# A Fourier neural operator and a dilation on one core: fc1 and fc2 of the head dealt out separately, and the fold, the rows and the first bursts in a new order

## The chip, the cores and the metric

The kernel runs on one core of one Trainium2 chip. The metric is device time in microseconds of one launch. PE is the matrix engine, DVE the vector engine, ACT the scalar engine, POOL and SP the engines that here mostly issue DMAs.

## The reference

The input x is eight images of 8 channels and 256 x 256 pixels, float32 throughout. Two layers, each with a residual:

```
x = x + conv(groupnorm(x))        # layer A: a grouped Fourier neural operator
x = x + dilate(groupnorm(x))      # layer B: the maximum over 3 x 3, padded with -2
```

`conv` has G = 4 groups. Two channels of a group and two coordinate planes go through a 1 x 1 convolution (fc0) to 10 channels. Four layers follow, each with a spectral convolution (rfft2, the lowest 12 x 12 modes mixed over channels, low and high rows apart, irfft2) plus a 1 x 1 convolution; the first three end in a swish. The head is fc1 (10 to 128 channels of a group), swish, fc2 (128 to 2).

## The kernel before

Images run one after the other. For an image, each of the four layers l = 0 to 3 is made of these stages:

- `spectrum_h`: the spectrum from the row transforms of the layer before (four DVE transposes, then the matmuls `p_b`). For layer 0 it is `spectrum_x`, on the raw image.
- `mix`: twelve DVE steps that multiply with the spectral weights (`load_sw`) and reduce, in pairs; then six short DVE operations fill `fs`, the fold's matmuls (`p_f`) fold the rows and DVE copies the result into `fz`.
- `rows_of`: three row groups (`p_g`), whose results DVE copies into `zt`.
- `layer`: eleven bursts (`p_z`), one for each chunk of the image: 48 instructions on PE that add the 1 x 1 convolution and the inverse transform of the columns, then two ACT passes that put swish of it into `h` (for l = 3 without swish; then the chunk also goes to HBM as `stored`). In layers 0 to 2 the new `h` is at once transformed for the next layer: `turn` (DVE transposes, two halves of a chunk), `transform` (64 matmuls `p_d` for two chunks, emptied by DVE and ACT) and `gather` (`p_u`, copied by DVE into `zt`).

The head reads `stored` back. It has 128 steps an image: `first(n)` is fc1 of 512 pixels (four matmuls in the program, eight instructions in the trace, then ACT passes of 512 and 1536 columns into one `act` buffer), and `second(n)` is fc2 of the two steps n and n + 1 (16 instructions into one bank), whose sum DVE adds to the image in `add`. The adds wait in `sums_due` until `sum_up` writes them out. After the last `add` of an image its dilation (`dilate`, or `dilate_last` for the last image) follows as tails.

The order on PE, DVE, ACT and SP is written by hand: it is the order in which the Python program issues instructions. `layers` is a generator that yields at chosen places, and the loop over the images puts work of the previous image's head or dilation there. Each head is a generator too: one `step()` of it is a `first(n)` and, when n is odd and over 2, `second(n - 3)`. A yield of `(1,)` deals one step and writes its add at once, `(1, 1)` two, `"late"` one step with the add left for the next, and `"tail"` a piece of the dilation. The head of an image thus runs beside the next image; the last image's head runs alone, with the dilation of the image before. The spectrum and mixing of layer 0 of the next image (`start`) are drawn piece by piece with `next(side, None)` during layer 3, and what is left of them is yielded by `rest`.

PSUM is shared by all through two tags, and a buffer is given again when all that read it are done:

```python
def ps_a(name):
    return ps.tile([128, 512], F32, tag="one", bufs=2, name=name)
def ps_tri(name):
    return ps.tile([128, 3, 512], F32, tag="tri", bufs=2, name=name)
```

`ps_four` takes one of each. A burst, a `first`, a `transform`, a fold and the first row group take both; the other row groups and the statistics of the dilation (`p_st_y`, `p_sv_y`) take a tri; `second`, `gather` and the rest take a one. The results of `first` go to four buffers:

```python
act = sb.tile([128, G, 512], F32, tag="act", bufs=4, name=f"act_{b}_{n}")
```

Image 0 has no head beside it (`alone[0]`), and there `copy` puts every second copy of `rows_of` on ACT.

Of the kernel before, what the change touches and what calls it, by code (L numbers as in the profile page):

```python
# [33 lines left out]
NBLK = 3  # L34
NCH = 11
NQ = 4
# [3 lines left out]
DR = 2  # L40
STEPS = 128


@with_exitstack
def fno_dilate_kernel(ctx: ExitStack, tc: tile.TileContext, a: dict, out: bass.AP):
# [304 lines left out]
    def spectrum_h(b, l, out_):  # L350
# [3 lines left out]
        for g in range(G):  # L354

            nc.vector.transpose(  # L356
                rows[:, 960 * g : 960 * (g + 1)].rearrange("p (i r) -> p i r", r=32), windows(g))
            yield (1,)
        yield (1,)
        p = ps_a(f"p_b_{b}_{l}")  # L360
# [25 lines left out]
    def mix(b, l, out_):  # L386
# [3 lines left out]
        for n in range(12):  # L390
# [5 lines left out]
            else:  # L396
# [25 lines left out]
        if l == 0:  # L422
            mr = out_["mr"]
            nc.vector.tensor_tensor(dc[:, 0:1], mr[:, 0:1], mr[:, 1:2], ALU.mult)
            out_["wcn"] = sb.tile([128, 32], F32, tag="wcn", bufs=1, name=f"wcn_{b}")
            nc.vector.tensor_scalar(out_["wcn"], wc, mr[:, 1:2], None, ALU.mult)
            for r in range(4):
                mm(one[part(r), n_f : n_f + NO * G], dc, wm[:, NO * r : NO * (r + 1), :], start=True, stop=True)
            nc.vector.tensor_tensor(
                fz[:, :, :, 24], one[:, n_f : n_f + NO * G].rearrange("p (o g) -> p o g", o=NO), cz[:, 0], ALU.add)  # L430
        else:
            nc.vector.tensor_copy(fz[:, :, :, 24], cz[:, l])
        if l < 2:
            nc.vector.tensor_copy(fz[:, :, :, 25], cz[:, 4 if l == 0 else 3])
        cols = fz.rearrange("p o g c -> p (o g) c")
        nc.vector.tensor_copy(
            cols[:, :, 0:6].rearrange("p x c -> p c x"), one[:, :n_f].rearrange("p (c x) -> p c x", c=6))
        for q in range(1, 4):
            nc.vector.tensor_copy(
                cols[:, :, 6 * q : 6 * q + 6].rearrange("p x c -> p c x"),  # L440
                tri[:, q - 1, :n_f].rearrange("p (c x) -> p c x", c=6))

    def rows_of(b, l, side):

        zv = zt[:, :, :, : NBLK * WID].rearrange("p r f (n o) -> p o n r f", n=NBLK)
        yield (1, 1)
        for oi in range(NO):
            name = f"p_g_{b}_{l}_{oi}"
            if oi == 0:
                banks = ps_four(name)[2]  # L450
            else:
                tri = ps_tri(name)
                banks = [tri[:, r, :] for r in range(3)]
# [4 lines left out]
            else:  # L458
                for g in range(G):
                    for j in range(NQ):  # L460
                        for r, p in enumerate(banks):
                            mm(p[part(j), NBLK * CS * g : NBLK * CS * (g + 1)], fz[part(r), oi, g, :],  # L462
                               rowg[part(r), :, j, :], start=True, stop=True)
            for r, p in enumerate(banks):
                src = p[:, : NBLK * CS * NQ]
                if l % 2 == 0:
                    dst = zv[:, NO * r + oi].rearrange("p n r f -> p n f r")
                    src = src.rearrange("p (n f r) -> p n f r", n=NBLK, r=CS)
                else:
                    dst = zv[:, NO * r + oi].rearrange("p n r f -> p f n r")  # L470
                    src = src.rearrange("p (f n r) -> p f n r", f=NQ, n=NBLK)
                copy(r, dst, src)
# [13 lines left out]
    def layer(b, l, out_, stored, side):  # L486
# [89 lines left out]
        for k in range((NCH + 1) // 2):  # L576
# [5 lines left out]
            if alone[0]:  # L582
# [5 lines left out]
                if pair:  # L588
                    turn(c + 1)
                continue  # L590
            if k == 1:
                transform(0)
            if k > 0:
                yield (1,)
            else:
# [15 lines left out]
        transform(k)  # L611
        yield (1,)
        gather(k)
# [7 lines left out]
    def rest(b, then):  # L621
        c = 0 if b == 0 else NCH - 4
        for n in then:
            yield n
# [78 lines left out]
    def head(b, stored, stats):  # L703
        hs, acts, box = {}, {}, {}
        last = b + 1 == n_img
# [22 lines left out]

        def first(n):

            sum_up()
            k, blk = n // 32 * NCH + n % 32 // NBLK, n % 32 % NBLK
            act = sb.tile([128, G, 512], F32, tag="act", bufs=4, name=f"act_{b}_{n}")
# [6 lines left out]

        def second(n):

            t, rb = n // 16, n % 16
            if rb == 8:
# [25 lines left out]

        load_state(0)
        yield
        load_state(1)
        load_y(0)
        yield
        load_state(2)
        yield
        for n in range(STEPS):
            if n % 32 % NBLK == 0:
                load_state(n // 32 * NCH + n % 32 // NBLK + 3)  # L780
            first(n)
            if n % 2 and n > 2:
                second(n - 3)
            yield
        second(STEPS - 2)
        sum_up()

# [58 lines left out]
    with tc.manual_schedule(engines={PE, DVE, ACT, SP}):  # L846
# [3 lines left out]
        for b in range(n_img):  # L850
            stored = [dram.tile([128, NQ * PIX], F32, tag=f"hs{c}", name=f"stored_{b}_{c}") for c in range(NCH)]
            ahead, new = {}, None
            for n in layers(b, stored, d, start(b + 1, ahead)):
                if n == "ready":
                    if new is None:
# [4 lines left out]
                        new = head(b, stored, stats_of[b])  # L860
                    next(new)
                elif n == "stored":
                    heads.append((b, new))
                    alone[0] = False
                elif n == "tail":
                    tail()
                elif heads:
                    for _ in range(1 if n == "late" else len(n)):
                        step()
                        if n != "late":  # L870
                            sum_up()
            d = ahead
        while step():
            sum_up()
            tail()
# [168 lines left out]
```

## Time and profile before

| what | us |
|---|---|
| median of three runs (lowest to highest) | 3849.73 (3849.6 to 3853.38) |
| the profiled execution, its own time | 3850.84 |
| span of the profiled execution, first to last instruction | 3849.0 |
| first row group of images 1, 2, 3, 4, 5, 6, 7 starts at | 357, 812, 1275, 1734, 2194, 2658, 3115 |
| last burst of layer 3 of image 7 starts at | 3546 |
| last fc2 starts at | 3820 |

An image in the middle takes about 460 us. Image 0 alone takes the first 340 us, the last image's head alone some 275, and DVE's last dilation and the output the rest. The mean granted clock of PE in the whole execution was 0.972. Line numbers in the views are those of the kernel before: L736 is fc1 and L751 fc2, L737 and L738 the two ACT passes of fc1, L542 and L545 the two halves of a burst, L550 and L552 its ACT passes, L510 transform, L524 gather, L493 turn, L760 the add. In the changed kernel fc1 is L752, fc2 L769 and the ACT passes L753 and L754.

### The profile page before, as it was taken

The numbers are of one execution on the slowest core, as the hardware profiler recorded it, in microseconds if no ns is written. First come the engines' busy times: TensorE is split into PE (matmuls) and PEld (weight loads), VectorE is DVE, ScalarE is ACT, GpSimd is POOL, SyncE is SP. The second block draws the span as 40 slices with busy tenths as digits, with TensorE's granted clock in tenths as the row PEclk, the third lists the DMA queues.
The fourth block names the chain that finished last, engine by engine and source line by source line (L and its number), as shares of the span: only waits on it lengthen the run. The fifth ranks groups of instructions, "written<-read, shape, count | busy, mean of one in ns | idle before, by whom it ended". The sixth has DMA issues, their size and how long they took to land.

```text
span 3849.0 us, 119276 instructions
## 1 busy us (share of the span) xinstructions
PE 3620.7 (94%) x54200; PEld 1347.2 (35%) x54200; DVE 2423.8 (63%) x3893; ACT 2832.3 (74%) x2919; POOL 117.0 (3%) x202
## 2 busy tenths in 40 slices
PE   5668999999999999999999999999999999999997
PEld 2333333333333333333333333333333333333222
DVE  6775665556775666766666676665676566673633
ACT  2435777777777777787777777777777777778986
POOL 1000000000000000000000000000000000000100
PEclk7878999999999999999999999999999999999998
DMA  3005111432225222361123612144222532225321
GB/s 88 15 28 193 48 47 45 150 107 61 65 85 178 77 61 61 99 200 55 49 64 110 193 56 58 44 145 154 61 63 59 178 99 63 65 64 182 114 54 51
DMA packets 114089, 345.11 MB, mean 90 GB/s; under 512 B 15984, under 2 KB 18480, under 8 KB 98160
## 3 DMA queue, kind: packets, MB, share of 16 engines
q1 hardware_dynamic: 95392, 276.32, 23.4%
q0 software_dynamic: 18192, 61.17, 5.0%
q8 instruction: 426, 6.98, 0.7%
q14 instruction: 79, 0.65, 0.1%
HBM read 213.43 MB, written 123.74 MB: 88 GB/s over the span
## 4 chain that ended last, share of the span: by engine, by line
PE 76%; DVE 14%; issue 5%; ACT 4%; DMA 1%; POOL 0%; DVEq 0%; POOLq 0%; ACTq 0%
PE p_fc L736 20%; PE p_fc L751 19%; PE p_z L545 10%; PE p_d L510 8%; PE p_z L542 8%; PE p_u L524 3%; PE p_z L539 3%; DVE S L397 3%; DVE turned L394 3%; PE p_b L366 2%; DVE y L760 2%; PE p_g L462 2%; ACT act L738 2%; DVE turned L356 1%; ACT act L737 1%
## 5 line engine op out<-in xcount | busy, mean ns | idle before, releaser
L738 ACT ACTIVATE act<-p_fc 128x1536 f32<-128x1536 f32 x1024 | 1492.6, 1458 | 36.1 <-PE p_fc L736 35.0
L736 PE MATMUL p_fc<-hs,c_w 32*128 32x512 f32 x8192 | 1227.4, 633 | 49.9 <-ACT act L738 13.5
L751 PE MATMUL p_fc<-act,c_w 128*32 128x512 f32 x8192 | 996.1, 602 | 2.0 <-issue 2.0
L737 ACT ACTIVATE act<-p_fc 128x512 f32<-128x512 f32 x1024 | 615.4, 601 | 360.1 <-PE p_fc L736 347.0
L493 DVE STREAM_TRANSPOSE turned<-h 128x1024 f32<-128x1024 f32 x528 | 633.9, 1226 | 250.7 <-ACT h L550 249.9
L550 ACT ACTIVATE h<-p_z 128x512 f32<-128x512 f32 (+1 forms) x528 | 511.9, 1022 | 265.4 <-PE p_z L545 265.4
L736 PEld LDWEIGHTS p_fc<-hs,c_w 32*128 32x128 f32 x8192 | 388.1, 185 | 666.4 <-ACT act L737 230.2
L760 DVE TENSOR_TENSOR y<-p_fc,y 128x512 f32<-128x512 f32 x392 | 267.1, 681 | 551.2 <-PE p_fc L751 551.2
L751 PEld LDWEIGHTS p_fc<-act,c_w 128*32 128x32 f32 x8192 | 215.6, 109 | 713.3 <-issue 376.3
L545 PE MATMUL p_z<-c_binv,zt 32*128 32x256 f32 x5632 | 415.5, 410 | 0.4
L542 PE MATMUL p_z<-h,c_wt 32*32 32x512 f32 x8448 | 367.3, 604 | 6.1 <-ACT act L737 4.2
L545 PEld LDWEIGHTS p_z<-c_binv,zt 32*128 32x128 f32 x5632 | 261.6, 189 | 312.8 <-issue 296.6
L510 PE MATMUL p_d<-turned,c_fw 32*32 32x480 f32 (+1 forms) x9216 | 308.6, 540 | 4.3 <-PE p_z L545 2.9
L514 ACT ACTIVATE turned<-p_d 128x1440 f32<-128x1440 f32 x144 | 182.9, 1270 | 95.2 <-PE p_d L510 92.0
L552 ACT ACTIVATE h<-p_z,c_bias 128x512 f32<-128x512 f32 (+1 forms) x176 | 186.5, 1110 | 76.0 <-PE p_z L545 75.8
L207 DVE COPY zt<-p_g 128x264 f32<-128x264 f32 x304 | 154.7, 604 | 76.6 <-PE p_g L462 46.5
L397 DVE TENSOR_REDUCE S<-turned 128x80 f32<-128x800 f32 x192 | 188.8, 983 | 5.7
L394 DVE TENSOR_TENSOR turned<-t,B 128x800 f32<-128x800 f32 x192 | 188.4, 981 | 0.1
L510 PEld LDWEIGHTS p_d<-turned,c_fw 32*32 32x32 f32 x9216 | 128.2, 103 | 170.2 <-issue 65.1
L356 DVE STREAM_TRANSPOSE turned<-zt 128x960 f32<-128x960 f32 x96 | 177.0, 1870 | 2.9 <-DVE zt L527 0.5
L542 PEld LDWEIGHTS p_z<-h,c_wt 32*32 32x32 f32 x8448 | 92.4, 103 | 188.8 <-ACT act L737 66.6
L524 PE MATMUL p_u<-turned,c_stack 128*32 128x480 f32 (+1 forms) x1152 | 136.7, 543 | 7.2 <-DVE turned L513 6.2
(182 smaller groups left out, 1742.8 us busy)
## 6 DMA issues: line engine op xcount, KB each, us to landing
stored<-h SPq DMA_DIRECT2D x88, 1024.0 KB
hs<-stored SPq DMA_DIRECT2D x352, 256.0 KB
t<-in_spw SPq DMA_DIRECT2D x96, 400.0 KB
yin<-y_rows POOLq DMA_DIRECT2D x56, 512.0 KB, 5.2
h<-in_xp SPq DMA_DIRECT2D x352, 48.0 KB
turned<-in_xw SPq DMA_DIRECT2D x16, 1024.0 KB
y<-in_x SPq DMA_DIRECT2D x56, 256.0 KB
y_rows<-y POOLq DMA_DIRECT2D x56, 256.0 KB, 3.9
```

What stands on the lines that cost most here:

```text
L394: nc.vector.tensor_tensor(pr, sw[k], bt[:, k2, k].unsqueeze(2).to_broadcast([128, G, 2 * WID, WID]), ALU.mult)
L397: nc.vector.tensor_reduce(s[k2][:, k].rearrange("p s o g -> p (s o) g"), pr.rearrange("p g m i -> p m g i"), AX.X, ALU.add,)
L493: nc.vector.transpose(dst[:, 2 * i : 2 * i + 2], h[:, c, 2 * i : 2 * i + 2].rearrange("p f (s x) -> p f s x", s=2))
L510: mm(banks[q][part(v % 4), : 240 * n], fw8[part(q), v, :], t[part(q), :, :, v, : NBLK * WID], start=v < 4, stop=v >= 4)
L542: mm(o, wt[part(q), l, g, :], h[part(q), c, f, :], start=True, stop=False)
L545: mm(banks[q][:, HW * s : HW * (s + 1)], zt[part(q), 2 * c + s].rearrange("p f o -> p (f o)"), binv[part(q), :], start=False, stop=s == 1)
L550: nc.scalar.activation(dst, src, AF.Silu)
L736: mm(banks[g], w1[part(g), blk, :], hs[k][part(g), :], start=True, stop=True)
L737: nc.scalar.activation(act[:, 0, :], one, AF.Silu)
L738: nc.scalar.activation(act[:, 1:4, :], tri, AF.Silu)
L751: mm(acc[part(g), :], w2[:, g, 15 - rb - i : 47 - rb - i], act[:, g, :], start=i == 0, stop=i == 1)
L760: nc.vector.tensor_tensor(y, sums, y, ALU.add)
```

## The change

What is dealt out is now a letter: `f` is one `first`, `c` one `second` with its add at once, `C` one `second` with its add left for the next `first`, and `t` a tail. A yield is a string of them. `head` returns functions and counters in place of a generator, and `step(kind)` goes to the first head in the list that still has work of that kind, so that at the switch `first` of the next image may come before the last `second` of the one before. The yields are written anew in `spectrum_h`, `mix`, `rows_of`, `layer` and `rest`. In `mix` and the fold one pair of fc1 and a fc2 now come before the fold's matmuls, the copies of `cz` go ahead of them, and three copies into `fz` become one. In `rows_of` the first row group's copies begin with the tri. In `layer`, bursts, turns and transform 0 of chunks 0 to 3 stand in another order. In layer 3, a chunk's letters are `ft` and `fc`. When all layers of the last image are done, the loop deals `f`, `f`, `c` and a tail until no head is left.

```diff
+REST = ("ff", "f", "f", "fC", "fc"), ("fC", "ffC", "ffC", "f", "fc")
...
# spectrum_h
-            yield (1,)
-        yield (1,)
+            yield "f" if g % 2 else "fc"
+        yield "fc"
# mix
-            if n not in (2, 6, 10) if l > 0 else n % 2 or n > 7:
-                yield "late"
+            if l == 0:
+                if n % 2 or n > 7:
+                    yield
+            elif n not in (2, 6, 10):
+                yield "fC" if n in (1, 4, 7, 9) else "f"
...
-        if l == 0:
-            yield "late"
+        yield "fc"
...
+        if l > 0:
+            nc.vector.tensor_copy(fz[:, :, :, 24], cz[:, l])
+        if l < 2:
+            nc.vector.tensor_copy(fz[:, :, :, 25], cz[:, 4 if l == 0 else 3])
         one, tri, banks = ps_four(f"p_f_{b}_{l}")
...
+        cols = fz.rearrange("p o g c -> p (o g) c")
+        nc.vector.tensor_copy(
+            cols[:, :, 6:24].rearrange("p x (q c) -> p q c x", q=3),
+            tri[:, :, :n_f].rearrange("p q (c x) -> p q c x", c=6))
...
-        for q in range(1, 4):
-            nc.vector.tensor_copy(
-                cols[:, :, 6 * q : 6 * q + 6].rearrange("p x c -> p c x"),
-                tri[:, q - 1, :n_f].rearrange("p (c x) -> p c x", c=6))
# rows_of
-        yield (1, 1)
+        yield "ffc"
...
-            for r, p in enumerate(banks):
-                src = p[:, : NBLK * CS * NQ]
+            n = NBLK * CS * NQ
+            for i, r in enumerate((1, 2, 3, 0) if oi == 0 else (0, 1, 2)):
+                src = banks[r][:, :n]
...
-            yield (1, 1) if oi == 0 else (1,)
-            if l == 3:
-                if oi != 1:
-                    next(side, None)
-            elif oi == 0:
-                yield "tail"
+            yield "fcf"[oi]
+            if l == 3 and oi != 1:
+                next(side, None)
+        if l < 3:
+            yield "t"
# layer, l == 3
                 burst(c)
-                yield (1,)
-                yield "tail"
+                yield "ft"
                 next(side, None)
                 if c + 1 < NCH:
-                    yield (1,)
+                    yield "fc"
                 if c < 8:
-                    yield "tail"
+                    yield "t"
                 next(side, None)
# layer, l < 3, after burst(c) and gather(k - 2)
+            if k == 0:
+                yield "t"
+                burst(1)
+                yield "f"
+                turn(0)
+                yield "cf"
+                continue
             if k == 1:
+                turn(1)
                 transform(0)
-            if k > 0:
-                yield (1,)
-            else:
-                yield "tail"
+                turn(2, (0,))
+                yield "fc"
+                turn(2, (1,))
+                yield "tf"
+                burst(3)
+                turn(3)
+                yield "t"
+                continue
+            yield "f"
             turn(c)
-            if k > 1:
-                transform(k - 1)
-            if k > 0:
-                for _ in range(2 if pair else 1):
-                    yield "tail"
+            transform(k - 1)
+            yield "tt" if pair else "t"
             if pair:
                 burst(c + 1)
                 turn(c + 1, (0,))
-            yield (1,)
+            yield "fc"
             if pair:
                 turn(c + 1, (1,))
...
-        yield (1,)
+        yield "f"
         gather(k)
# dealing out
-    def step():
-
-        if not heads:
-            return False
-        b, gen = heads[0]
-        if next(gen, b) is b:
-            heads.pop(0)
-            tails.append((dilate if b + 1 < n_img else dilate_last)(b, stats_of.pop(b)))
-            return step()
-        return True
+    def step(kind):
+
+        for i, (b, (done, first, second, _)) in enumerate(heads):
+            if kind == "f" and done[0] < STEPS:
+                return first()
+            if kind != "f" and 2 * done[1] < STEPS:
+                second()
+                if kind == "c" or 2 * done[1] == STEPS:
+                    sum_up()
+                if 2 * done[1] == STEPS:
+                    heads.pop(i)
+                    tails.append((dilate if b + 1 < n_img else dilate_last)(b, stats_of.pop(b)))
+                return
# the end
-        while step():
-            sum_up()
+        while heads:
+            for kind in "ffc":
+                if heads:
+                    step(kind)
             tail()
```

More of the change, by code (lines that the diff above doesn't have):

```diff
@@ L428, in mix @@
                 mm(one[part(r), n_f : n_f + NO * G], dc, wm[:, NO * r : NO * (r + 1), :], start=True, stop=True)
+        cols = fz.rearrange("p o g c -> p (o g) c")
+        nc.vector.tensor_copy(
+            cols[:, :, 6:24].rearrange("p x (q c) -> p q c x", q=3),
+            tri[:, :, :n_f].rearrange("p q (c x) -> p q c x", c=6))
+        nc.vector.tensor_copy(
+            cols[:, :, 0:6].rearrange("p x c -> p c x"), one[:, :n_f].rearrange("p (c x) -> p c x", c=6))
+        if l == 0:
             nc.vector.tensor_tensor(
                 fz[:, :, :, 24], one[:, n_f : n_f + NO * G].rearrange("p (o g) -> p o g", o=NO), cz[:, 0], ALU.add)
-        else:
[L432 to L435, printed above, removed]
-        nc.vector.tensor_copy(
-            cols[:, :, 0:6].rearrange("p x c -> p c x"), one[:, :n_f].rearrange("p (c x) -> p c x", c=6))
-        for q in range(1, 4):
-            nc.vector.tensor_copy(
-                cols[:, :, 6 * q : 6 * q + 6].rearrange("p x c -> p c x"),
-                tri[:, q - 1, :n_f].rearrange("p (c x) -> p c x", c=6))
     def rows_of(b, l, side):
         zv = zt[:, :, :, : NBLK * WID].rearrange("p r f (n o) -> p o n r f", n=NBLK)
-        yield (1, 1)
+        yield "ffc"
         for oi in range(NO):
@@ L449, in rows_of @@
             if oi == 0:
-                banks = ps_four(name)[2]
+                one, tri, banks = ps_four(name)
             else:
@@ L471, in rows_of @@
                     src = src.rearrange("p (f n r) -> p f n r", f=NQ, n=NBLK)
-                copy(r, dst, src)
-            yield (1, 1) if oi == 0 else (1,)
-            if l == 3:
-                if oi != 1:
-                    next(side, None)
-            elif oi == 0:
-                yield "tail"
+                copy(i, dst, src)
+            yield "fcf"[oi]
[3 more added lines that the diff above has]
+            yield "t"
     def read_x(b, c):
@@ L590, in layer @@
                 continue
+            if k == 0:
[5 more added lines that the diff above has]
+                continue
             if k == 1:
+                turn(1)
                 transform(0)
-            if k > 0:
-                yield (1,)
-            else:
-                yield "tail"
-            turn(c)
-            if k > 1:
-                transform(k - 1)
-            if k > 0:
-                for _ in range(2 if pair else 1):
-                    yield "tail"
+                turn(2, (0,))
[7 more added lines that the diff above has]
+            yield "f"
+            turn(c)
+            transform(k - 1)
+            yield "tt" if pair else "t"
             if pair:
@@ L622, in rest @@
         c = 0 if b == 0 else NCH - 4
-        for n in then:
-            yield n
+        for n, _ in enumerate(then):
+            yield REST[b > 0][n]
             for _ in range(2 if b == 0 else 1):
@@ L703, in head @@
     def head(b, stored, stats):
-        hs, acts, box = {}, {}, {}
+        hs, acts, box, done = {}, {}, {}, [0, 0]
         last = b + 1 == n_img
@@ L727, in load_y, with first @@
                     y, a["x"][b].rearrange("c (p t s w) -> (c p) t s w", p=16, t=8, s=2)[:, t])
-        def first(n):
+        def first():
+            n = done[0]
+            done[0] += 1
             sum_up()
+            if n % 32 % NBLK == 0:
+                load_state(n // 32 * NCH + n % 32 // NBLK + 3)
             k, blk = n // 32 * NCH + n % 32 // NBLK, n % 32 % NBLK
@@ L739, in first, with second @@
             acts[n] = act
-        def second(n):
+        def second():
+            n = 2 * done[1]
+            done[1] += 1
             t, rb = n // 16, n % 16
@@ L769, in add, with ahead @@
                     bass.AP(whole.tensor, whole.offset + (1 + 2 * t) * HW, [[16 * HW, 128], [HW, 2], [1, HW]]), y)
[L771 to L785, printed above, removed]
-        sum_up()
+        def ahead(n):
+            load_state(n)
+            if n == 1:
+                load_y(0)
+        return done, first, second, ahead
     def dilate(b, stats):
@@ L851, in fno_dilate_kernel @@
             stored = [dram.tile([128, NQ * PIX], F32, tag=f"hs{c}", name=f"stored_{b}_{c}") for c in range(NCH)]
-            ahead, new = {}, None
+            ahead, new, n_ready = {}, None, 0
             for n in layers(b, stored, d, start(b + 1, ahead)):
@@ L860, in fno_dilate_kernel @@
                         new = head(b, stored, stats_of[b])
-                    next(new)
+                    new[3](n_ready)
+                    n_ready += 1
                 elif n == "stored":
@@ L864, in fno_dilate_kernel @@
                     alone[0] = False
[L865 to L871, printed above, removed]
+                else:
+                    for kind in n or "":
+                        if kind == "t":
+                            tail()
+                        elif heads:
+                            step(kind)
             d = ahead
-        while step():
-            sum_up()
+        while heads:
+            for kind in "ffc":
+                if heads:
+                    step(kind)
             tail()
```

## The prediction

> **What bounds the kernel now.** I read the page from the top, then the timelines of PE and ACT in three places. The first lines give the bound.
>
> ```profile
> PE 3620.7 (94%) x54200; PEld 1347.2 (35%) x54200; DVE 2423.8 (63%) x3893; ACT 2832.3 (74%) x2919; POOL 117.0 (3%) x202
> ...
> PEclk7878999999999999999999999999999999999998
> PE 76%; DVE 14%; issue 5%; ACT 4%; DMA 1%; POOL 0%; DVEq 0%; POOLq 0%; ACTq 0%
> ```
>
> PE is the bound in all but the first slices and the last, and the chain of waits runs along it for 76%. The change removes no matmul: only PE's waits can shrink or grow. What makes PE wait is PSUM. There are two buffers of three banks ("tri") and two of one bank ("one"); a burst, an fc1 step (`first`), a transform and a row group each take the next of both or of tri, and must wait until the user before the last one has been emptied by ACT or DVE. An fc2 pair (`second`) takes only a "one". So the order in which these stand decides what is hidden. For the changed kernel that order is read from its built program; 1024 fc1 steps and 512 fc2 pairs stand in both.
>
> The second view is PE in a chunk of layer 3, then ACT in the same stretch:
>
> ```profile
> 1707.61 1.04 PE L736 MATMUL p_fc<-hs,c_w 32*128 32x512 f32 x8
> 1708.58 1.92 PE L751 MATMUL p_fc<-act,c_w 128*32 128x512 f32 x16
> 1710.47 1.14 PE L736 MATMUL p_fc<-hs,c_w 32*128 32x512 f32 x8
> 1711.54 1.42 PE L542 MATMUL p_z<-h,c_wt 32*32 32x512 f32 x32
> 1712.89 1.15 PE L545 MATMUL p_z<-c_binv,zt 32*128 32x256 f32 x16
> 1713.85 1.04 PE L736 MATMUL p_fc<-hs,c_w 32*128 32x512 f32 x8
> ```
>
> ```profile
> 1707.81 2.12 ACT L552 ACTIVATE h<-p_z,c_bias 128x512 f32<-128x512 f32 x2 [0.40 <-PE p_z L545]
> 1709.82 0.60 ACT L737 ACTIVATE act<-p_fc 128x512 f32<-128x512 f32 x1
> 1710.30 1.46 ACT L738 ACTIVATE act<-p_fc 128x1536 f32<-128x1536 f32 x1
> ```
>
> The chunk is burst, fc1, fc2, fc1: 6.24 us from 1707.61 to 1713.85. The burst's tri is emptied at 1707.81 + 2.12 = 1709.93, and the second fc1, which reuses it, starts at 1710.47: hidden, because the fc2 (1.9 us) lies between.
>
> The third is ACT, then PE, in the last image's head, which stands alone at the end:
>
> ```profile
> 3709.09 1.47 ACT L738 ACTIVATE act<-p_fc 128x1536 f32<-128x1536 f32 x1
> ...
> 3714.70 0.60 ACT L737 ACTIVATE act<-p_fc 128x512 f32<-128x512 f32 x1 [0.32 <-PE p_fc L736]
> 3715.19 1.45 ACT L738 ACTIVATE act<-p_fc 128x1536 f32<-128x1536 f32 x1
> ```
>
> ```profile
> 3707.59 1.92 PE L751 MATMUL p_fc<-act,c_w 128*32 128x512 f32 x16
> 3709.45 2.31 PE L736 MATMUL p_fc<-hs,c_w 32*128 32x512 f32 x16
> 3711.68 1.93 PE L751 MATMUL p_fc<-act,c_w 128*32 128x512 f32 x16
> 3713.54 2.03 PE L736 MATMUL p_fc<-hs,c_w 32*128 32x512 f32 x16
> 3715.49 1.92 PE L751 MATMUL p_fc<-act,c_w 128*32 128x512 f32 x16
> ```
>
> Two fc1 and one fc2 take (3715.49 - 3707.59)/2 = 3.95 us. One more price comes out of it: an ACT pass over a tri ends at 3709.09 + 1.47 = 3710.56, and the fc1 that waited for it makes room for the fc2 at 3711.68, 1.12 later.
>
> **Layer 3 (a loss).** Now a chunk is "ft", "fc": burst, fc1, fc1, fc2. Three tri users a chunk on two buffers mean that the second fc1 takes the tri of its own burst. Counted from the first fc1: tri empty at 0.20 + 2.12 = 2.32, second fc1 done at 2.32 + 1.12 = 3.44, fc2 at 5.30 (1.86 each), next burst 2.05 (its slot where it waits for nothing): 7.35 us. The ten chunks of before take 61.8 us without the small matmuls of `spectrum_x` (mean 6.18), so 1.17 more each. These small ones stand behind the fc2 as before and cost the same. Queued behind the waiting fc1 are the fc2 and the next burst, and ACT then waits for that burst. Only if ACT were the bound itself would it cost nothing; its passes take about 6 us a chunk, so it isn't. Ten chunks: +11.7 an image.
>
> **Before layer 3's first burst (a gain).** Between fold and rows the trace shows fc1 slots of 1.90, 2.04 and 1.5 us where 1.07 is the plain slot: they wait for ACT or for the copies of `p_g`. Now an fc1 pair and an fc2 (4.0 us) stand between the last mixing step and the fold, and one fc1 fewer among the row groups. Walked through with plain slots (fc1 1.07, fc2 1.85, fold 0.80, row group 1.11, copies of three banks 1.4), with the four `bn_x` of 2.4 us still ahead of the second group's copies, layer 3 reaches its first chunk 1.8 us sooner at equal work. Net of layer 3: about +9.6 an image (+11.7 - 1.8, and a little rounding).
>
> **Layers 1 and 2, fold to transform 1.** Same order as above, then bursts 0 and 1, fc1, fc2, fc1, burst 2, transform 0, fc1, fc2, fc1, bursts 3 and 4. Walked in layer 1 from the start of the last fc2 of mixing (1388.0): fold at 5.9, row groups 11.0, 13.7 and 16.7, bursts 19.4, 21.7 and 27.8, transform 0 at 29.9, bursts 36.0 and 38.1. Burst 4 started at 41.1, so it comes 3.0 us earlier; in layer 2, whose waits were longer, 4.0. But most is given back: burst 3 now stands directly before burst 4, and all of `turn(3)` comes after it. On DVE there follow two transposes (2.35 us), a dilation step (1.4) and only then the copy of `p_u` (0.65), and transform 1 waits for both, with burst 5 behind it. In layer 1: burst 3 emptied at 1428.15, plus 4.4 is 1432.6, against this row:
>
> ```profile
> 1433.30 2.19 PE L510 MATMUL p_d<-turned,c_fw 32*32 32x480 f32 x58
> ```
>
> Gain 0.6; in layer 2 by the same sum 1.75. If DVE weren't late it would be 3.0 and 4.0; if the dilation step fell worse, zero.
>
> **Switch and layer 0.** From the last burst of layer 3 to transform 1 of layer 0 before takes 60.6 to 65.2 us (mean 63.6); the differences go with half clock:
>
> ```profile
> 1752.00:1759.00 7.00, 7.00 (x56) 2.66 (x72) 3.75 (x4) 3.77 (x4) 0.00 (x0) 0.58 0.15 40
> ```
>
> The columns are the stretch, busy time of PE, its weight loads, DVE, ACT and POOL, then granted clock, DMA share and GB/s. The clock is 0.58, just after burst 1 had waited 1.7 us for burst 0 (with `p_st_y` between them both tri are taken; this wait stays). The new order walks through in 59.2 at full clock. I take half of the old clock loss (3.0 us) as still there: 60.6, a gain of 3.0, between 1.4 (no clock won) and 4.4. The overlap of the heads puts two fc1 between the old head's last two fc2, which stood back to back; that is in the walk.
>
> **Small edits.** Joining three `fz` copies saves 0.14 each on DVE beside PE; `copy` with the tri first frees it 0.46 sooner and is in the walk. Image 0 alone: same instructions, below 1 us either way. The copies from `cz` now stand ahead of the fold's matmuls, 0.17 each while PE runs an fc2. No DMA is added; on SP's queue the loads of `hs` and `y` move with their step by one step at most (2 us), and `hs` is asked for nine steps ahead (18 us at 1.98 a step). Tails stay at 11 a layer, with POOL's DMAs.
>
> **The end (the largest term).** After the last layer the loop deals "ffc". It begins when one fc1 of image 6 is left, so the letters run out of step: fc1 14, then fc2 of 10 and 11, where before fc2 10 came after fc1 13. `act` has four buffers, so ACT's pass over fc1 14 must wait for fc2 10, its reader, which PE now runs after fc1 14. In the built program ACT's wait for that step names the fc2's last matmul. Counted from an fc2's start: it ends at 1.92; ACT's first pass starts at 1.94, its tri pass at 2.43 (0.49 later, as 3714.70 to 3715.19) and ends at 3.88; behind it waits the pass over fc1 15, on PE fc1 15 waits for its one and fc1 16 for its tri, and the next fc2 starts 1.12 after that tri is free: 5.00 us a round against 3.95. From fc2 0 to fc2 124 are 62 rounds. Before they take 258.0 us (13 of it late `add`s behind DVE's dilation, which the longer round half hides: 6 left). After: 310 + 6 = 316, so +58; from 45 (a round of 4.8, all late adds hidden) to 70 (nothing hidden). The same wait at the switch of image 6 to 7 costs 3 more.
>
> A rule here is in the Trainium skill, "Perfetto Trace Analysis", Matmuls: independent groups should rotate through banks so that emptying one overlaps the next group's matmuls. The new chunk of layer 3 breaks it, and by the rule alone the chunk would be slower too, without an amount. "TensorE: Matmul & The Clock Gate", in its table for kernels, holds gaps under about 3 us harmless for the clock; the row with 0.58 after a wait of 1.7 speaks against it. By the rule the end keeps full clock and the sum stands; by the row, with a tenth of the end at half clock, it would be an estimated 25 more.
>
> **Sum.** The profiled execution took 3850.84 (span 3849.0), 1.1 above the median of 3849.73. Seven images have a head beside them: 7 x (9.6 - 0.6 - 1.75 - 3.0) = +30. End +58 + 3. Total +91, less about 3 for image 1's first steps: 3939, or 3938 against the median. Own range 3905 to 3972: windows +-15, layer 3 +-14, end +-13.
>
> **Rivals.**
> - The windows close entirely (the faster side): every wait of PE between the last mixing step and transform 1, and at the switch, goes, and DVE's chain is never late. Work against elapsed time there gives at most 4.8 (layer 1), 5.9 (layer 2), 13 (switch and layer 0) and 3.2 (layer 3's rows), 27 an image. It decides once over (82 + 61)/7 = 20 an image are won. At 27: 3851 + 143 - 188 = 3806. Against it: the transposes, 1.2 us each, haven't moved off DVE. 0.06.
> - The end's wait isn't there, or ACT has slack for it: 3938 - 61 = 3877, still slower. For it: ACT is only 7.1 of 7.8 us busy there; against it: its buffer wait lies in a ring with PE. 0.10.
> - Layer 3's chunk stays at 6.2: 3938 - 82 = 3856, at the edge of no change. 0.07.
>
> The forecast has 0.77. A difference under 0.2% (8 us) can't be told here from none. Faster 0.06; same 0.03; slower 0.91. The range takes in the second rival: 3877 to 3972.
>
> **What would show it.** Right: chunks of layer 3 of 7.3 us with fc1 slots of 2.4; at the end fc2 every 5.0 us, and ACT's L753 released by fc2 (L769) instead of fc1. Wrong: fc2 at the end every 4 us, chunks near 6.2, or transform 1 of layers 1 and 2 starting over 2 us earlier than I say.

## The result and the profile after

The changed kernel takes 3911.4 us (median of four runs, 3904.1 to 3914.06). Beside it the kernel before took 3849.66 (four runs, 3845.29 to 3853.38). The ratio is 1.0158, 95% interval 1.014 to 1.0175. Forecast were 3938 with a range of 3877 to 3972, and slower at 0.91. The time is in the range, 27 us under the forecast, and the parts show that this is the sum of a large miss and a smaller one on the other side.

The profiled execution has a span of 3908.7 us. From its page, the busy times and the first line of the chain of waits:

```profile
PE 3641.7 (93%) x54200; PEld 1363.0 (35%) x54200; DVE 2417.6 (62%) x3829; ACT 2821.1 (72%) x2919; POOL 117.0 (3%) x202
...
PE 79%; DVE 12%; ACT 5%; issue 3%; DMA 0%; DVEq 0%; POOL 0%; POOLq 0%; ACTq 0%
```

PE's 54200 instructions are the same and it is still the bound; its share of the chain rose from 76% to 79%. Of the 59.7 us between the two spans, 38.7 are more idle time of PE (267.0 against 228.3) and 21.0 are more busy time for the same instructions. To see where they lie, I cut both traces at the same marks on PE and took the mean of images 2 to 7:

| stretch on PE, us | before | after | difference | the prediction's term |
|---|---|---|---|---|
| last burst of layer 3 to transform 1 of the next image's layer 0 | 63.62 | 58.97 | -4.65 | -3.0 |
| on to transform 1 of layer 1 | 117.06 | 118.91 | +1.85 | -0.6 |
| on to transform 1 of layer 2 | 116.55 | 116.04 | -0.51 | -1.75 |
| on to the first burst of layer 3 | 95.39 | 94.20 | -1.19 | with the next: +9.6 |
| first to last burst of layer 3 | 66.91 | 79.23 | +12.32 | |

One fc1 (1.07 us) has moved from the fourth stretch to the first, so at equal work these two are -5.7 and -0.1. The sum is +7.8 an image, 46.9 in six images. Images 0 and 1 add 3.1, the last switch 1.6 (14.24 to 15.81 from the last burst to the first fc2 of image 7), the end 8.7 (258.02 to 266.68 from fc2 0 to fc2 124), and the rest after it -0.6: 59.7 in all, as between the two spans.

PE's timeline in a chunk of layer 3, where the prediction showed the burst, fc1, fc2, fc1 of before:

```profile
1718.75 1.16 PE L545 MATMUL p_z<-h,c_wt 32*32 32x512 f32 x32
1719.84 1.15 PE L548 MATMUL p_z<-c_binv,zt 32*128 32x256 f32 x16
1720.80 2.06 PE L752 MATMUL p_fc<-hs,c_w 32*128 32x512 f32 x10
1723.17 1.13 PE L752 MATMUL p_fc<-hs,c_w 32*128 32x512 f32 x6 [0.31 <-ACT h L555]
1724.23 1.93 PE L769 MATMUL p_fc<-act,c_w 128*32 128x512 f32 x16
1726.09 1.16 PE L545 MATMUL p_z<-h,c_wt 32*32 32x512 f32 x32
```

```profile
1721.00 2.12 ACT L555 ACTIVATE h<-p_z,c_bias 128x512 f32<-128x512 f32 x2 [1.57 <-PE p_z L548]
```

From burst to burst 7.34 us. The row "x10" is the first fc1 (eight instructions) and two of the second, which went to the one bank; the other six need the tri and start at 1723.17, when ACT's L555 has emptied the burst (1721.00 + 2.12 = 1723.12). In the list of waits this is PE's weight loads, "L752 <- ACT h L555", 145.0 us in 156 places.

PE and ACT at the end, where only the last image's head runs:

```profile
3702.47 1.92 PE L769 MATMUL p_fc<-act,c_w 128*32 128x512 f32 x16
3704.33 2.46 PE L752 MATMUL p_fc<-hs,c_w 32*128 32x512 f32 x16
3706.72 1.92 PE L769 MATMUL p_fc<-act,c_w 128*32 128x512 f32 x16
```

```profile
3703.67 0.60 ACT L753 ACTIVATE act<-p_fc 128x512 f32<-128x512 f32 x1 [0.48 <-PE p_fc L769]
3704.16 1.45 ACT L754 ACTIVATE act<-p_fc 128x1536 f32<-128x1536 f32 x1
3705.49 0.60 ACT L753 ACTIVATE act<-p_fc 128x512 f32<-128x512 f32 x1
```

ACT's L753 is released by fc2 (L769), as forecast. But it starts at 3703.67, 1.20 after the fc2's start, and not at its end (3704.39). A round is 3706.72 - 3702.47 = 4.25, not 5.00. By the prediction's own signs the end is thus nearer to wrong (a fc2 every 4 us) than to right (every 5.0).

PE and DVE at transform 1 of layer 1, image 3, where the copy of `p_u` (L530) was forecast to be late behind `turn(3)` (L496, two transposes in a row) and a dilation step (L825 to L832):

```profile
1432.34 1.14 PE L752 MATMUL p_fc<-hs,c_w 32*128 32x512 f32 x8
1435.68 2.31 PE L513 MATMUL p_d<-turned,c_fw 32*32 32x480 f32 x48 [2.21 <-DVE zt L530]
```

```profile
1431.26 2.37 DVE L496 STREAM_TRANSPOSE turned<-h 128x1024 f32<-128x1024 f32 x2 [2.04 <-ACT h L553]
...
1434.37 0.69 DVE L832 TENSOR_TENSOR o<-o,yin 128x512 f32<-128x512 f32 x1
1434.98 0.65 DVE L530 COPY zt<-p_u 128x480 f32<-128x480 f32 x1
```

DVE runs without a break from 1431.26 to 1435.63, and PE stands for 2.21 us. Before, the fc1 ahead of transform 1 (which started at 1433.30) had its plain slot of 1.07; now that slot is 3.35.

```profile
1432.22 1.14 PE L736 MATMUL p_fc<-hs,c_w 32*128 32x512 f32 x8
```

### The profile page after: what moved, and what is told of

Read it like the earlier page. It is cut to its first block, busy times and chain, and to the rows that moved or that the text cites. A ratio compares the mean times of both kernels' runs of the same rounds, so it can differ in the third digit from the quotient of the medians.

```text
span 3908.7 us, 119331 instructions
## 1 busy us (share of the span) xinstructions
PE 3641.7 (93%) x54200; PEld 1363.0 (35%) x54200; DVE 2417.6 (62%) x3829; ACT 2821.1 (72%) x2919; POOL 117.0 (3%) x202
## 4 chain that ended last, share of the span: by engine, by line
PE 79%; DVE 12%; ACT 5%; issue 3%; DMA 0%; DVEq 0%; POOL 0%; POOLq 0%; ACTq 0%
PE p_fc L769 22%; PE p_fc L752 21%; PE p_z L548 9%; PE p_d L513 8%; PE p_z L545 7%; ACT h L555 4%; PE p_z L542 3%; PE p_u L527 3%; PE p_b L367 2%; DVE S L398 2%; DVE y L778 2%; DVE turned L395 2%; PE p_g L465 2%; DVE turned L357 1%; DVE zt L208 1%
## 5 line engine op out<-in xcount | busy, mean ns | idle before, releaser
L752 PE MATMUL p_fc<-hs,c_w 32*128 32x512 f32 x8192 | 1237.2, 629 | 47.0 <-ACT h L555 24.3
L769 PE MATMUL p_fc<-act,c_w 128*32 128x512 f32 x8192 | 990.1, 600 | 4.8 <-issue 4.8
L753 ACT ACTIVATE act<-p_fc 128x512 f32<-128x512 f32 x1024 | 615.7, 601 | 397.2 <-PE p_fc L752 350.4
L496 DVE STREAM_TRANSPOSE turned<-h 128x1024 f32<-128x1024 f32 x528 | 633.3, 1226 | 256.3 <-ACT h L553 256.3
L778 DVE TENSOR_TENSOR y<-p_fc,y 128x512 f32<-128x512 f32 x392 | 268.4, 685 | 645.9 <-PE p_fc L769 645.9
L752 PEld LDWEIGHTS p_fc<-hs,c_w 32*128 32x128 f32 x8192 | 405.2, 184 | 686.0 <-ACT act L753 180.6
L769 PEld LDWEIGHTS p_fc<-act,c_w 128*32 128x32 f32 x8192 | 214.5, 109 | 688.9 <-issue 325.5
L545 PE MATMUL p_z<-h,c_wt 32*32 32x512 f32 x8448 | 358.9, 612 | 9.5 <-DVE y L778 8.4
L513 PE MATMUL p_d<-turned,c_fw 32*32 32x480 f32 (+1 forms) x9216 | 317.9, 560 | 31.7 <-DVE zt L530 31.0
L555 ACT ACTIVATE h<-p_z,c_bias 128x512 f32<-128x512 f32 (+1 forms) x176 | 186.5, 1110 | 165.4 <-PE p_z L548 165.2
L398 DVE TENSOR_REDUCE S<-turned 128x80 f32<-128x800 f32 x192 | 188.9, 984 | 5.9
L395 DVE TENSOR_TENSOR turned<-t,B 128x800 f32<-128x800 f32 x192 | 188.3, 981 | 0.1
```

The source lines that it names most:

```text
L398: nc.vector.tensor_reduce(s[k2][:, k].rearrange("p s o g -> p (s o) g"), pr.rearrange("p g m i -> p m g i"), AX.X, ALU.add,)
L496: nc.vector.transpose(dst[:, 2 * i : 2 * i + 2], h[:, c, 2 * i : 2 * i + 2].rearrange("p f (s x) -> p f s x", s=2))
L513: mm(banks[q][part(v % 4), : 240 * n], fw8[part(q), v, :], t[part(q), :, :, v, : NBLK * WID], start=v < 4, stop=v >= 4)
L545: mm(o, wt[part(q), l, g, :], h[part(q), c, f, :], start=True, stop=False)
L555: nc.scalar.activation(dst, src, AF.Identity, bias=bias3)
L752: mm(banks[g], w1[part(g), blk, :], hs[k][part(g), :], start=True, stop=True)
```

## The experiments

All ratios are to the kernel before, run on the same chip. The marks are those of the table above.

**Layer 3's chunk alone put back.**

```diff
-                yield "ft"
+                yield "fct" if c + 1 < NCH else "ft"
                 next(side, None)
                 if c + 1 < NCH:
-                    yield "fc"
+                    yield "f"
```

> The changed kernel with layer 3's chunk back in its old order (burst, fc1, fc2, fc1); all else as changed. Theory (the second fc1 of a chunk waits for ACT's pass over its own burst): chunks fall from 7.38 to about 6.2 us, the fc1 slot from 2.50 to about 1.1, and the time by 7 images x 10 chunks x 1.13 = 79 us, from 3911 to about 3832 (ratio to the kernel before 0.995). Rival (ACT or DVE bounds layer 3 by itself, the order only moves the wait): chunks stay at 7.0 or more, 3890 to 3911.

Measured: 3850.18, ratio 1.000 (0.999 to 1.001). The ten chunks are back: 66.86 from first to last burst against 79.23, so the wait for the chunk's own burst was all of that loss and the rival is out. Seven images of that are 86 us, yet only 61 came. 33 were lost in one place (8 came back in other windows): the switch and layer 0 rose from 58.97 to 64.54 in each of six images, on the same order of PE. PE there, then DVE:

```profile
1701.84 1.14 PE L752 MATMUL p_fc<-hs,c_w 32*128 32x512 f32 x8
1706.05 1.42 PE L752 MATMUL p_fc<-hs,c_w 32*128 32x512 f32 x8 [3.08 <-DVE y L778]
1707.40 3.29 PE L769 MATMUL p_fc<-act,c_w 128*32 128x512 f32 x16
```

```profile
1703.40 0.98 DVE L395 TENSOR_TENSOR turned<-t,B 128x800 f32<-128x800 f32 x1
1704.41 0.99 DVE L398 TENSOR_REDUCE S<-turned 128x80 f32<-128x800 f32 x1
1705.32 0.68 DVE L778 TENSOR_TENSOR y<-p_fc,y 128x512 f32<-128x512 f32 x1
```

The L395 and L398 are the next image's mixing: five such pairs stand without a break from 1695.72 to 1705.40, and the add (L778) of an fc2 that had ended at 1701.90 waits behind them; its bank is what PE waits for. After the 3.08 us the fc2 takes 3.29 instead of 1.92, and the granted clock from 1705 to 1711 is 0.72. The wait is 3.08 in five of the six images (1.23 in image 2). In the changed kernel, at the same switch, it is 0.67:

```profile
1735.25 1.14 PE L752 MATMUL p_fc<-hs,c_w 32*128 32x512 f32 x8 [0.67 <-DVE y L778]
```

There only four of the pairs stand in a row ahead of the add. With the slow chunks DVE was that far ahead, so the switch's gain in the changed kernel was partly paid for in layer 3.

**The adds at the switch ahead of the mixing**, on the kernel just shown.

```diff
-REST = ("ff", "f", "f", "fC", "fc"), ("fC", "ffC", "ffC", "f", "fc")
+REST = ("ff", "f", "f", "fC", "fc"), ("ffc", "ffC", "f", None, "fc")
 # rest
+        if b > 0:
+            yield "fc"
         for n, _ in enumerate(then):
             yield REST[b > 0][n]
```

> The changed kernel with layer 3's chunk in its old order, as run before, and at the switch the add of the old head's last steps put ahead of the next image's mixing on DVE (the letters of each step are dealt before its DVE work instead of after it, and the first two fc2 are summed at once); PE's order is that of the run before. Theory (with faster chunks the mixing on DVE is still running at the switch, the add of fc2 124 stands behind it and the next head's first fc1 waits 3.2 us for it, the fc2 behind at half clock): the fc1 slot of 4.2 us goes to 1.8, switch and layer 0 from 65.1 to about 61, 6 x 3.8 = 23 us: 3850 - 23 = 3827 (ratio 0.994). Rival (DVE's mixing itself is late, so the fold behind it waits instead): about 3850.

Measured: 3812.0, ratio 0.9895 (0.9879 to 0.9911), 38 less where 23 were expected. Switch and layer 0 fell from 64.54 to 59.92: 4.6 in each of six images is 28, with the same order of fc1 and fc2 on PE at these switches and only DVE's adds moved, so the late add is shown to be the cause of 4.6 of the 5.6 us. Another 15 I had not foreseen: `rest` deals its new first letters for the last image too, where no mixing follows, and that put the end's letters in step; the end went from 266.63 to 253.82 and the way to it from 16.07 to 13.65. (Up to the last burst of image 1 it took 5 more, 4 of them in image 0, which has no head beside it and whose order is the same.)

**The end in step.**

```diff
+        step("f")
+        step("c")
         while heads:
             for kind in "ffc":
```

> The changed kernel with one fc1 and one fc2 dealt just before the last image's head is left alone, so that the letters of the end stand in step (fc2 n after fc1 n+3, as before the change). Theory (ACT's pass over fc1 n+4 waits only for the first half of fc2 n, which costs 0.2 to 0.3 us a round): rounds go from 4.25 to about 4.0 us, the end from 266.7 to about 258, and the start of the end gives 1.5 back: about 3901 (ratio 1.013). Rival, my recorded step (that wait is worth 1.05 us a round, and something else hid it): 3850 (ratio 1.000). Second rival (the end's length is set by late adds, not by the order): 3911.

Measured: 3892.67, ratio 1.0111 (1.0097 to 1.0126). The end took 255.21 instead of 266.68, the way to it 13.39 instead of 15.81: 13.9 less. That is most of the 19 that the time fell; 3 more lie in windows whose order is the same. The recorded step would have given 3850 and is out.

**The end's order kept, with six `act` buffers for the last image.**

```diff
-            act = sb.tile([128, G, 512], F32, tag="act", bufs=4, name=f"act_{b}_{n}")
+            if last and n % 6 > 3:
+                act = spare[:, 16512 + 2048 * (n % 6 - 4) : 16512 + 2048 * (n % 6 - 3)].rearrange(
+                    "p (g w) -> p g w", g=G)
+            else:
+                act = sb.tile([128, G, 512], F32, tag="act", bufs=4, name=f"act_{b}_{n}")
```

> The changed kernel, where the last image's head has six act buffers instead of four (two more in the space of h, which is free by then); no order is changed. Theory (at the end ACT's pass over fc1 n+4 waits for the first half of fc2 n to free its act buffer, which makes a round 4.25 us): that wait goes, ACT's first pass follows its fc1, rounds 4.0 to 4.1, the end from 266.7 to 253 to 258 us: 3900 (ratio 1.013). Rival (the order of the letters alone, by PSUM, makes the round): 3911. Second rival, my recorded step (1.05 us a round): 3850.

Measured: 3895.9, ratio 1.0115 (1.01 to 1.0129); the end 252.85. No order was changed, so the buffer is the cause. ACT's waits between 3620 and 3780 us, first in the changed kernel, then with six buffers (fc1 is L756 there, ACT's pass L757):

```profile
ACT act L753 <- PE p_fc L769: 20.5, 37, 2.7
```

```profile
ACT act L757 <- PE p_fc L756: 5.5, 14, 0.9
ACT h L757 <- PE p_fc L756: 6.8, 8, 2.7
```

The columns are us in total, times, and the longest; "h" stands for the two added buffers, which lie in the space of `h`. The wait for fc2 is gone, and what is left is a wait for fc1, 12.3 us in 22 places. In the kernel before it was 16.3 in 25. The mechanism of my end was right, its price not.

**The first bursts of layers 0 to 2 in the old order**, the fold and rows as changed.

```diff
+            if k == 0 and not alone[0]:
+                yield "f"
             burst(c)
...
             if k == 0:
                 yield "t"
-                burst(1)
-                yield "f"
                 turn(0)
-                yield "cf"
+                burst(1)
+                turn(1, (0,))
+                yield "fc"
+                turn(1, (1,))
                 continue
             if k == 1:
-                turn(1)
                 transform(0)
-                turn(2, (0,))
-                yield "fc"
-                turn(2, (1,))
-                yield "tf"
+                yield "f"
+                turn(2)
+                yield "tt"
                 burst(3)
-                turn(3)
-                yield "t"
+                turn(3, (0,))
+                yield "fc"
+                turn(3, (1,))
                 continue
```

> The changed kernel with the first bursts, their turns and transform 0 of layers 0 to 2 in the old order; the fold, the row groups and layer 3 as changed. Theory (the new first-burst order loses what the rows gain, because transform 1 waits for all four transposes and the copy of p_u): layers 1 and 2 each reach transform 1 about 2 us sooner (2.4 and 1.7 an image), fc1 slots of 3.3 before it go to about 1.1, 7 x 4.1 = 28 us less: about 3883 (ratio 1.009). Rival (the copy of p_u and the tail on DVE are late in any order): 3905 to 3915. Second rival (the new burst order is what gained in layer 0): 3911 + 7 x 3 = 3930.

Measured: 3899.32, ratio 1.0135 (1.012 to 1.0149): 12 less, not 28. Layers 1 and 2 did what the theory said: 116.86 and 113.32 against 118.91 and 116.04, and the fc1 ahead of transform 1 in layer 1 is back at 1.07. But layer 0 went the other way, 62.61 against 58.97. There the new order gains, which the second rival had in part.

**The same in layers 1 and 2 only.** The changed kernel's two branches stay for layer 0, ahead of the old ones:

```diff
-            if k == 0 and not alone[0]:
+            if k == 0 and l > 0 and not alone[0]:
                 yield "f"
...
+            if l == 0 and k == 0:
+                yield "t"
+                burst(1)
...
+            if l == 0 and k == 1:
+                turn(1)
+                transform(0)
...
```

> The changed kernel with the first bursts in the old order in layers 1 and 2 only; layer 0 keeps the new one. Theory (the new order wins in layer 0, where the run before showed 62.3 us from the switch to transform 1 in the old order against 59.1, and loses in layers 1 and 2): layer 0 stays at 59, layers 1 and 2 as in the run with all first bursts old (22.7 and 22.5 us from burst 0 to transform 1 against 26.1 and 26.0): 3899 - 6 x 3.2 = 3880 (ratio 1.008). Rival (the 3.2 us in layer 0 is half clock that falls somewhere else in each run): about 3899.

Measured: 3883.82, ratio 1.0083 (1.007 to 1.0095). Layer 0 is 59.63, layers 1 and 2 are 116.74 and 113.23. The theory holds: the new order of the first bursts is a gain in layer 0 and a loss in the other two.

**The first row group's copies in the old order.**

```diff
-            for i, r in enumerate((1, 2, 3, 0) if oi == 0 else (0, 1, 2)):
+            for i, r in enumerate((0, 1, 2, 3) if oi == 0 else (0, 1, 2)):
```

> The changed kernel with the copies of the first row group in the old order (the single bank first, then the three banks of the tri). Theory (the tri is free one copy, 0.46 us, sooner with the tri first, and the fc1 behind the group waits for it): the fc1 slot behind the first row group goes from 1.56 to 1.77 by that copy, to about 2.0 to 2.2, 28 groups beside a head: up to 28 x 0.46 = 13 us more, 3915 to 3924 (ratio 1.0165 to 1.019). Rival (that fc1 waits for the single bank, or what is lost there is won back at the next group): 3911.

Measured: 3921.15, ratio 1.0184 (1.017 to 1.0198), some 10 more than the changed kernel. The fc1 behind the group went from 1.56 to 1.97 in layer 2 and from 1.77 to 2.17 in layer 1 (image 4): the 0.41 is seen in the slot itself. Against the scatter of the windows the 10 us alone would be weak: 3 of them lie in the last switch and the end, where there is no row group.

**The three losses undone together** (layer 3, the end, all first bursts).

> All three edits together: layer 3's chunk and the first bursts in their old orders, the end in step; fold, row groups, head steps and switch as changed. Theory (the three losses are independent): 3911 - 79 - 10 - 28 = 3794 (ratio 0.9855). Rival (waits taken away in one place come back in the next, or half clock eats them): 3820 to 3850.

Measured: 3821.51, ratio 0.9921 (0.9907 to 0.9936). The rival was right: the switch and layer 0 took 66.37, the longest of all kernels, with the late add and the old bursts on top of each other.

**What the runs pointed to** (old chunk in layer 3, old first bursts in layers 1 and 2, adds ahead of the mixing, and the two extra steps ahead of the end).

> What the runs so far point to, together: new fold, rows, switch and layer 0; old first bursts in layers 1 and 2; old chunk of layer 3; the end in step; the add ahead of the mixing at the switch. Theory (the parts are independent once the add is out of the way): 3911 - 61 - 19 - 31 - 23 = 3777 (ratio 0.981). Rival (layer 3's and the first bursts' gains are given back at the switch, as in the run with all three edits): 3815 to 3822.

Measured: 3794.11, ratio 0.9852 (0.9835 to 0.9868), 17 over the theory. 10 of these are the end, 263.52: put in step twice, it was out again on the other side. Without the two extra steps:

```diff
-        step("f")
-        step("c")
         while heads:
```

> As the last combination, but without the two extra steps ahead of the end (the steps dealt at the switch are dealt for the last image too, so that the end already stood in step and those two put it out again, to the other side). Theory: the end goes from 263.5 back to 253.8 us, the last image's switch gives 1.2 of it back: 3794 - 10 = 3784 (ratio 0.983). Rival (the end's length depends on where DVE's dilation steps fall, not on the step between fc1 and fc2): 3790 to 3800.

Measured: 3783.28, ratio 0.9833 (0.9819 to 0.9846). The end is 253.89 as expected. This version beats both kernels; it keeps the new fold, rows, switch and layer 0.

**One fc1 moved in between the row groups of layers 1 and 3**, on that version.

```diff
-        yield "ffc"
+        yield "ffc" if l % 2 == 0 else "fc"
...
-            yield "fcf"[oi]
+            yield "fcf"[oi] if l % 2 == 0 else ("ff", "c", "f")[oi]
```

> The kernel of the run beside it, with one fc1 of layers 1 and 3 moved from before the first row group to between the first and the second; the number of instructions is the same. In the traces so far PE stands still in the row groups of layers 1 and 3 with nothing awaited but its own instructions: 19.7 us in 19 places in the changed kernel, 6.1 in 5 before, 17.0 in 19 in the last combination. Theory (640 instructions of three row groups come too close together for the instruction queue, which brings 256 at a time): those waits fall to under 8 us, 9 us less and up to 5 more through the clock: 3784 - 12 = 3772 (ratio 0.980). Rival (the wait is set by the total of instructions, or by the data transfers beside it, not by the spacing): within 4 us of 3784.

Measured: 3785.01, ratio 0.9841 (0.9827 to 0.9854): no gain. The waits went from 18.8 us in 19 places to 15.8 in 13, fewer but longer. The theory, that this much spacing would do, fell.

**Six `act` buffers for the last image, as above, on the kernel just before.**

> The kernel of the run beside it with six act buffers for the last image's head. Theory (with the letters in step ACT waits for PE's fc2 no longer, so more buffers bring little): the end from 253.8 to 250 to 254, within 4 us of the run beside it. Rival (the ring of act buffers still costs 0.1 to 0.15 a round): 8 us less.

Measured: 3785.47, ratio 0.9839 (0.9825 to 0.9852); the end 253.85 against 253.89. With the letters in step the ring costs nothing.

## Why the prediction was right, and where it was not

- **Sign and mechanism.** All three waits that I named as new are in the trace, released by what I said: the chunk of layer 3 by its own burst, transform 1 by the copy of `p_u`, ACT at the end by fc2. Undone one by one, each gave time back. That the forecast lies only 27 us off is in part luck: the next points show 49 us too much at the end and 23 too little in the windows.
- **Layer 3's chunk, 7.35: measured 7.34 in the rows shown, 7.38 on average.** This term carried the verdict: without it the two kernels are equal (ratio 1.000). The rival of 3856 had it the other way.
- **The step that failed: "ACT's wait for that step names the fc2's last matmul".** From it I took a start at 1.94 after the fc2's, and a round of 5.00. In the trace the pass starts at about 1.2 in all 62 rounds. The records of the first eight of the fc2's 16 matmuls end at 1.07, and these are the ones that read the `act` buffer of step n; the other eight read that of n + 1. The rest of the chain was right: 1.20 + 0.49 + 1.45 + 1.11 = 4.25. Over 62 rounds that is 263.5 us, with 3.2 of late rounds on top where 6 were reckoned, and +58 became +8.7. The bounds for this term don't come out of its own numbers either: 62 rounds of 4.8 are 298 us, so +40 and not +45, and 310 + 13 gives +65 and not +70; the 8.7 is far below both. At the end the granted clock was 1.00, so the 25 that the prediction would have added for half clock did not come either. The rival in which the end's wait is absent (3877) was nearer in its term; but the wait was there.
- **The windows were too cheap by 23 us: +30, less 3 for image 1, against +50.0.** Layers 1 to 3 were worse than said by 2.45, 1.24 and (at equal work) 2.6 an image, the switch and layer 0 better by 2.7 at equal work. In layer 1 burst 0 to transform 1 takes 26.1 us, where the prediction's walk has 25.2 and the kernel before 23.0: the wait was nearly sized. But the stretch behind transform 1 was taken as unchanged, and it isn't: the clock falls there. Ten us of the changed kernel from transform 1 of layer 1 on, then the same stretch of before:

```profile
1435.00:1445.00 10.00, 9.32 (x168) 3.65 (x168) 5.12 (x7) 5.34 (x6) 1.29 (x2) 0.83 0.33 99
```

```profile
1435.00:1445.00 10.00, 10.00 (x180) 3.72 (x168) 5.39 (x8) 7.78 (x9) 0.00 (x0) 1.00 0.07 19
```

  The third number from the end is the granted clock: 0.83 after the wait of 2.21 us, 1.00 where there was none. In images 2 to 7 there are 12 such waits in layers 1 and 2, of 2.08 to 2.21 us; in the ten us behind them the clock is 0.83 for nine and 1.00 for three. In the kernel before, and in the run with the old first bursts in layers 1 and 2, there is no such wait and it is 1.00 in all 12. Up to the next layer's `p_b` this makes 1.2 us an image more behind layer 1 and 0.9 behind layer 2. Behind layer 0's transform 1 the clock is 1.00, so the clock is worth about as much as layer 2's miss, a third of layer 3's and none of layer 1's. In layer 1, 0.9 is the walk just named, and the rest lies in the fold and the rows.

  The prediction had weighed the table for kernels of "TensorE: Matmul & The Clock Gate" of the Trainium skill, which asks for no idle gaps of PE over about 3 us, and had taken shorter ones to be harmless by it. These waits of 2.1 to 2.2 us speak against that. The row of 0.58 that the prediction set against it does not: in the 7 us ahead of that row PE is busy throughout, and its timeline shows no wait of 1.7 us. What lowered the clock there stays open.

```profile
1745.00:1752.00 7.00, 7.00 (x104) 2.64 (x100) 2.83 (x8) 3.88 (x4) 0.00 (x0) 0.93 0.01 2
```

- **The switch was better for a reason that I had not written.** I put its gain down to the order of PE. The runs show that DVE's mixing, which had more time beside the slower chunks, was part of it: 5.6 us an image came back as loss once the chunks were fast, and 4.6 of these went again with the add ahead of the mixing. Neither the gain nor the loss of the two parts can be added up without the other.
- **Fold and rows won in layer 2 and hardly in layers 1 and 3.** In the run with the old first bursts in layers 1 and 2, only the fold, the rows and the letters around them differ there from the kernel before: layer 2 is 3.3 shorter (113.23 against 116.55), layer 1 only 0.3 (116.74 against 117.06), and before layer 3's first burst it is 1.1 at equal work (93.24 against 95.39, less the fc1 moved), where I had said 1.8. Part of what is missing is in the last section. A small edit brought nothing: the joined `fz` copies were to save 0.14 each, but the three took 0.55 in a row (L439, before) and the one takes 0.54 (L437):

```profile
1392.44 0.55 DVE L439 COPY fz<-p_f 128x72 f32<-128x72 f32 x3
```

```profile
1397.30 0.54 DVE L437 COPY fz<-p_f 128x216 f32<-128x216 f32 x1
```

## What to carry to other kernels

The wait for a buffer ended here with the last instruction that reads that buffer, not with the group that it stands in: price such a wait from the moment in the group at which the reading stops, and check that against one row where the same kind of wait already occurs. Where work of one engine is spread beside a stretch of another, the slowness of the stretch is a resource: making it faster moves the spread work (here mixing on DVE) behind the next point of use, so the two have to be moved together. Give a result its place in the queue ahead of the long work that doesn't need it.

## What the runs showed of the hardware that I had not expected

PE waited for its own instructions. In the trace such idle time is put down to "issue". From PE's timeline of the changed kernel in the row groups of layer 1, image 4, then the whole kernel's row in the list of waits, after and before:

```profile
1875.35 0.88 PE L465 MATMUL p_g<-c_rowg,fz 32*32 32x66 f32 x67
1877.98 0.42 PE L465 MATMUL p_g<-c_rowg,fz 32*32 32x66 f32 x29 [1.75 <-issue]
```

```profile
PE p_g L465 <- issue: 19.4, 20, 1.8
```

```profile
PE p_g L462 <- issue: 8.7, 7, 1.8
```

A row group stops after 67 of its 96 matmuls for 1.75 us, though the profile shows nothing else that it waits for. After 400 us, with the few that fall on fc1 or fc2 beside the row groups, PE lost 6.1 us in 5 such places before and 19.7 in 19 after. The records of the instruction queue (426 transfers of 16384 bytes, which the page lists as q8) point to why: in all 24 places PE goes on between 1.26 and 1.57 us after one of these blocks has landed, and so does it here, 1876.48 to 1877.98. (With a block every 9.0 us, an estimated 3% of the places would fall there by chance.) The three row groups of layers 1 and 3 hold 640 instructions (320 matmuls and their weight loads), and the new order has them within 9.2 us, this wait included, where the old took 12.2 (1857.47 to 1869.64); those of layers 0 and 2 are ten matmuls in the program. The 13.6 us more may be a good part of what the new rows should have won in layers 1 and 3. That the density of the order is the cause isn't shown: one fc1 in between changed nothing in the time, and no run thinned the instructions out. The Trainium skill, "Runtime: NRT & Kernel Launch", section on instruction fetch mechanics, states the blocks of 16 KiB, as seen here, and calls their cost mostly hidden; beside this kernel's many small matmuls PE stood for the 19.7 us just counted.
